# VectorE's 32x32 block transposes for the input rows and the first layer's row terms, in a two-layer graph-attention and expert kernel

## The chip, the cores and the metric

The kernel runs on one core of one Trainium2 chip, as one launch. The metric is device time in microseconds, first instruction to last; lower is better. A core has five engines that each run their own list of instructions in order and wait for one another through semaphores: TensorE (PE in the profile, with PEld for its weight loads), VectorE (DVE), ScalarE (ACT), GpSimd (POOL) and SyncE (SP), which here only issues DMAs.

## The reference: what is computed

`x` has 64 batches of 256 rows and 256 columns in f32; `adj` is one 256x256 mask for all of them. Each batch goes through two layers:

```python
# layer 0
x = x + elu(gat4(layernorm(x), adj, W0, a0))     # 4 heads of 64, slope 0.2
x = x + layernorm(x) @ weight.T + bias
# layer 1
x = x + relu(gat1(layernorm(x), adj, W1, a1))    # 1 head of 256, slope 0.01
x = x + moe(layernorm(x))                        # 8 experts, the best 2 of each row
```

Attention of a head, with `q = h @ W`:

```python
e = leaky_relu((q @ a_src)[:, None] + (q @ a_dst)[None, :])   # one term per row, one per column
p = softmax(where(adj, e, -inf), axis=-1)
out = p @ q
```

The expert stage adds `moe(n) = n + sum of the two chosen experts' gelu(n @ w1 + b1) @ w2 + b2`, each weighted by its share.

## The kernel before

**Layout.** Rows lie on the 128 partitions: a batch is a tile of 128 partitions, 2 row halves (NT) and 256 columns. A matmul needs its contracted dimension on the partitions, so before every projection the batch is transposed to 2 column halves (KT) on partitions by 256 rows.

**One batch** (`batch_layers`, L370). It takes its rows from `xin`, issues the load of the batch three further on (`load_batch`, L93, one 256 KB DMA on SyncE's queue), takes statistics (`norm_stats`, L286: VectorE's mean and variance, then GpSimd's `rstd`), and transposes (`transposed`, L297: four 128x128 transposes on TensorE into a PSUM bank, which ScalarE copies out at L305). `projected` (L308) multiplies with `wx0`; the centring of the layer norm is folded into the weights, and `rstd` comes in afterwards as a scale. Each head has three more columns beside its 64 (columns 64 to 66): the attention terms. L323 takes their exponentials on ScalarE, L327 scales q on VectorE.

**Scores without a softmax pass.** `scores` (L333) uses that an exponential of a sum is a product and a leaky ReLU is a maximum, so that a score before normalisation is `max(row term, column term) * mask`, the other factors being in q or cancelling. The row term must run along the free dimension, the same on all partitions. L339 gets it by transposing column `d+1` of q, broadcast to 128 columns, on TensorE: 8 transposes a batch in layer 0 (4 heads, 2 halves), 2 in layer 1. L346 makes `z` from it on VectorE. Layer 0 does two heads in one step, two in the next. `attended` (L352) multiplies `z` with q on TensorE and divides by the sum, which is q's extra column.

**The rest of the batch.** elu and the residual (L394 to L398, `ex` and `x1`), the linear layer (L401 to L417, with `x1b` as residual plus bias), the second attention (L420 to L434, with `rel`), the last norm, and the router's logits (L472). Rows go to `xs` in DRAM by expert through indirect DMAs on GpSimd (`send`, L739, `route`, L758), come back in pairs of tiles (`expert_pair`, L584), pass two matmuls (`hidden`, `result`) and are added to `out` by indirect DMAs (`scatter`, L675).

**What sets the order.** The program order is written out by hand (L898 on). A batch is a generator that yields a rank; a step of the outer loop runs one piece of every active job, sorted by rank. A batch starts every third step, so about six are in flight, and what one piece makes is mostly used in the next step. Every engine keeps that order. In ranks: the load, the statistics of x0 and its transpose are at 40; the projection at 20; heads 0 and 1 at 10; heads 2 and 3 at 10; `attended` at 50. Expert pieces come at 90, 40, 30 and 80, indirect DMAs at 95 and 97.

**Buffers.** The eight PSUM banks are handed out in turn by `bank` (L78). SBUF tiles share slots by tag: `e`, `x1b` and `rel` have two each, `xT` four, `xin` six.

Of the kernel before, what the change touches and what calls it, by code (L numbers as in the profile page):

```python
# [26 lines left out]
def kernel(  # L27
# [69 lines left out]
        )  # L97
        return t

    AHEAD = 3  # L100
    xin = {0: load_batch(0)}


# [3 lines left out]
    nc.vector.memset(ones, 1.0)  # L107
    mean_w = const.tile([P, P], F32, tag="mean_w", name="mean_w")
    nc.vector.memset(mean_w, 1.0 / D)
    mhalf = const.tile([P, NT], F32, tag="mhalf", name="mhalf")  # L110
    nc.vector.memset(mhalf, -0.5)

# [26 lines left out]
    def gnn_weights(w, a, heads, slope, name):  # L139

        d = D // heads
        wx = const.tile([P, KT, heads, d + 3], F32, tag=name, name=name)
        for k in range(KT):
            nc.sync.dma_start(
                out=wx[:, k, :, :d],  # L150
                in_=w[k * P : (k + 1) * P, :].rearrange("p (h d) -> p h d", h=heads),
            )
        av = work.tile([P, 2, d], F32, tag="e", name=name + "_a")
        nc.scalar.dma_start(out=av.rearrange("p s d -> p (s d)"), in_=rows_to_all(a, 2 * d))
        prod = work.tile([P, heads, d], F32, tag="hp", name=name + "_p")
        for k in range(KT):
            for s, c in ((0, d + 1), (1, d)):
                nc.vector.tensor_mul(
                    prod, wx[:, k, :, :d], av[:, s : s + 1, :].to_broadcast([P, heads, d])
                )  # L160
                nc.vector.tensor_reduce(wx[:, k, :, c : c + 1], prod, AX.X, ALU.add)
            nc.vector.tensor_scalar(
                wx[:, k, :, d + 1 : d + 2], wx[:, k, :, d + 1 : d + 2], 1.0 - slope, None,
                op0=ALU.mult,
            )
            nc.vector.tensor_scalar(
                wx[:, k, :, d + 2 : d + 3], wx[:, k, :, d : d + 1], slope - 1.0, None,
                op0=ALU.mult,
            )
        flat = wx.rearrange("p k h c -> p k (h c)")  # L170
        center(flat, heads * (d + 3))
        return flat
# [2 lines left out]
    wx1 = gnn_weights(w1g, a1g, 1, SLOPE1, "wx1")  # L175

    wf_in = work.tile([P, KT, D], F32, tag="xT", name="wf_in", bufs=4)
    xin.update({b: load_batch(b) for b in range(1, AHEAD)})
    nc.scalar.dma_start(out=wf_in, in_=wf.rearrange("(t p) i -> p t i", p=P))
    wfT = const.tile([P, KT, D], F32, tag="wfT", name="wfT")  # L180
# [10 lines left out]
    nc.scalar.dma_start(out=bias_f, in_=rows_to_all(bf, D))  # L191
    nc.vector.tensor_scalar(bias_f, bias_f, -1.0, None, op0=ALU.add)

    r_in = work.tile([E, D], F32, tag="x1b", name="r_in")
    nc.scalar.dma_start(out=r_in, in_=router)
    rT = const.tile([P, KT, E], F32, tag="rT", name="rT")
    pr = bank("pr", [KT, E])
# [132 lines left out]
            )  # L330
        return q

    def scores(q, heads, hs, mask, probs):  # L333

        d = D // heads
        pd = bank("pd", [len(hs), N])
        for i, h in enumerate(hs):
            for t in range(NT):
                nc.tensor.transpose(  # L339
                    pd[:, i, t * P : (t + 1) * P],  # L340
                    q[:, t, h, d + 1 : d + 2].to_broadcast([P, P]), ident,
                )
        for i, h in enumerate(hs):
            z = work.tile([P, NT, N], F32, tag="z", name="z", bufs=6)
            for j in range(NT):
                nc.vector.scalar_tensor_tensor(  # L346
                    z[:, j, :], pd[:, i, :], q[:, j, h, d + 2 : d + 3], mask[:, j, :],
                    op0=ALU.max, op1=ALU.mult,
                )
            probs.append(z)  # L350
# [19 lines left out]
    def batch_layers(b, c0, xng, lg):  # L370

        x0 = xin.pop(b)
        if b + AHEAD < B:
            xin[b + AHEAD] = load_batch(b + AHEAD)
        _, rstd = norm_stats(x0)
        xT = transposed(x0)
        yield 20
        q = projected(xT, wx0, H, rstd)
        yield 10
        probs = []  # L380
        scores(q, H, range(0, 2), masks[0], probs)
        yield 10
        scores(q, H, range(2, 4), masks[0], probs)
        yield 50
        pvs, rinv = attended(q, H, probs)
        hp = work.tile([P, NT, D], F32, tag="hp", name="hp")
        for t, pv in enumerate(pvs):
            nc.vector.tensor_tensor(
                hp[:, t, :].rearrange("p (h d) -> p h d", h=H), pv[:, :, :HD],
                rinv[:, t, :, None].to_broadcast([P, H, HD]), ALU.mult,  # L390
            )
        yield 20
        ex = work.tile([P, NT, D], F32, tag="e", name="e")
        nc.scalar.activation(ex, hp, AF.Exp)  # L394

        x1 = work.tile([P, NT, D], F32, tag="x1", name="x1", bufs=2)
        nc.vector.scalar_tensor_tensor(x1, hp, 0.0, x0, op0=ALU.max, op1=ALU.add)
        nc.vector.scalar_tensor_tensor(x1, ex, 1.0, x1, op0=ALU.min, op1=ALU.add)  # L398
        yield 30
        x1b = work.tile([P, NT, D], F32, tag="x1b", name="x1b")  # L400
        nc.gpsimd.tensor_add(x1b, x1, bias_f[:, None, :].to_broadcast([P, NT, D]))  # L401
        _, rstd = norm_stats(x1)
        xT = transposed(x1)
        yield 70
        pf = bank("pf", [NT, D])
        for t in range(NT):
            for k in range(KT):
                nc.tensor.matmul(  # L408
                    pf[:, t, :], xT[:, k, t * P : (t + 1) * P], wfT[:, k, :],
                    start=(k == 0), stop=(k == KT - 1),  # L410
                )
        x2 = work.tile([P, NT, D], F32, tag="x2", name="x2", bufs=4)
        for t in range(NT):
            nc.vector.scalar_tensor_tensor(
                x2[:, t, :], pf[:, t, :], rstd[:, t : t + 1], x1b[:, t, :],
                op0=ALU.mult, op1=ALU.add,
            )  # L417
        _, rstd = norm_stats(x2)
        yield 60
        xT = transposed(x2)  # L420
        yield 20
        q = projected(xT, wx1, 1, rstd)
        yield 10
        probs = []
        scores(q, 1, range(1), masks[1], probs)
        yield 40
        pvs, rinv = attended(q, 1, probs)
        yield 5
        rel = work.tile([P, NT, D], F32, tag="rel", name="rel")
        for t, pv in enumerate(pvs):  # L430
            nc.scalar.activation(  # L431
                rel[:, t, :], pv[:, 0, :D], AF.Relu, scale=rinv[:, t, :]
            )
        nc.gpsimd.tensor_add(x2, x2, rel)  # L434
        yield 60
        mv, rstd = norm_stats(x2)
        yield 15

        by = small.tile([P, 2, NT], F32, tag="by", name="by")
        nc.vector.scalar_tensor_tensor(  # L440
            by[:, 0], mv[:, :, 0], -1.0, rstd, op0=ALU.mult, op1=ALU.mult
        )
        nc.vector.tensor_scalar(by[:, 1], rstd, 1.0, None, op0=ALU.add)
        yield 50
        xe = keep.tile([P, NT, ROW], F32, tag="xng", name="xng", bufs=XNG)
        dense = b >= ROUTED
        base = work.tile([P, NT, D], F32, tag="dbase" if dense else "base", name="base")
        for t in range(NT):
            nc.scalar.activation(
                xe[:, t, :D], x2[:, t, :], AF.Identity, bias=by[:, 0, t : t + 1],  # L450
                scale=rstd[:, t : t + 1],
            )
        for t in range(NT):
            nc.scalar.activation(
                base[:, t, :], x2[:, t, :], AF.Identity, bias=by[:, 0, t : t + 1],
                scale=by[:, 1, t : t + 1],
            )
        xng.append(xe)
        yield 35
        if not dense:  # L460
            d = nc.sync.dma_start(
                out=out_rows[b * N : (b + 1) * N, :].rearrange("(t p) d -> p t d", p=P), in_=base
            )
            tc.declare_no_dep(
                d.ins, query=SYNC, group="out", reason="no row is added to before its chunk has been sent"
            )
            tc.add_to_no_dep_group("out", d.ins)
            based.append(d.ins)
            nc.sync.nop()
        xT = transposed(xe[:, :, :D], *(("xTd", DENSE) if dense else ()))  # L470
        yield 50
        pl = bank("pl", [NT, E])  # L472
        for t in range(NT):
            for k in range(KT):
                nc.tensor.matmul(
                    pl[:, t, :], xT[:, k, t * P : (t + 1) * P], rT[:, k, :],
                    start=(k == 0), stop=(k == KT - 1),
                )
        nc.vector.tensor_copy(lg[:, c0 : c0 + NT, :], pl)
        if dense:  # L480
            dense_batch[b] = dict(base=base, xT=xT)
# [480 lines left out]
```

## Time and profile before

| | |
|---|---|
| median of three runs | 1795.14 us |
| lowest, highest | 1784.11, 1803.95 us |
| profiled execution | 1821.2 us |
| granted TensorE clock in it | 0.937 of full |
| DMA | 192.90 MB in 137374 packets, mean 106 GB/s |

The profile's rows and the shares below are from the execution of 1821.2 us. A row of its costliest groups reads: line, engine, operation, tile written and tiles read, shape, count; then busy time and mean length in ns; then the idle time of the engine ahead of these instructions and what ended it. Groups that the change touches (total busy time, and mean length of one):

| line | engine | what | count | busy us | mean ns |
|---|---|---|---|---|---|
| L301 | PE | transposes of x0 (`pt<-ident,xin`) | 256 | 39.8 | 280 |
| L301 | PE | transposes of x1, x2 and the normed rows | 768 | 119.8 | 277 |
| L339 | PE | transposes of the row terms, both layers | 640 | 106.0 | 281 |
| L305 | ACT | copies of the transposed rows | 256 | 144.9 | 589 |
| L346 | DVE | z | 640 | 265.1 | 473 |

Busy times of TensorE are sums of overlapping records; what a group of them takes in the engine's order has to be read from start to start in the timeline. Three stages follow one another: until about 270 us batches with little expert work beside them, until about 1450 us batches and experts together, then experts alone.

### The profile page before, as it was taken

The numbers are of one execution on the slowest core, as the hardware profiler recorded it, in microseconds if no ns is written. First come the engines' busy times: TensorE is split into PE (matmuls) and PEld (weight loads), VectorE is DVE, ScalarE is ACT, GpSimd is POOL, SyncE is SP. The second block draws the span as 40 slices with busy tenths as digits, with TensorE's granted clock in tenths as the row PEclk, the third lists the DMA queues.
The fourth block names the chain that finished last, engine by engine and source line by source line (L and its number), as shares of the span: only waits on it lengthen the run. The fifth ranks groups of instructions, "written<-read, shape, count | busy, mean of one in ns | idle before, by whom it ended". The sixth has DMA issues, their size and how long they took to land. (4 is left out here: it accounts for less than half of the span.)

```text
span 1821.2 us, 30155 instructions
## 1 busy us (share of the span) xinstructions
PE 1629.5 (89%) x9254; PEld 1433.0 (79%) x9254; DVE 1231.4 (68%) x4680; ACT 839.9 (46%) x1773; POOL 1084.2 (60%) x1164
## 2 busy tenths in 40 slices
PE   6998889899999999999999999999989998778692
PEld 5787778788888888888878788887878887667582
DVE  6889887867685858686766768688678876522231
ACT  1243333355554555554545545555455545443241
POOL 1333645557575767767676757576685767644444
PEclk9999989899998999998989999999899989889897
DMA  4410211235344444544354534444353436576663
GB/s 137 140 36 24 71 60 53 79 109 121 105 95 104 109 126 108 132 103 110 93 119 112 119 91 95 118 111 128 84 127 101 107 82 166 118 186 139 135 139 43
DMA packets 137374, 192.90 MB, mean 106 GB/s; under 512 B 18680, under 2 KB 91392, under 8 KB 137216
## 3 DMA queue, kind: packets, MB, share of 16 engines
q1 hardware_dynamic: 86592, 122.61, 22.0%
q0 software_dynamic: 49632, 67.39, 20.6%
q8 instruction: 76, 1.25, 0.3%
q10 hardware_dynamic: 992, 0.99, 0.2%
q14 instruction: 82, 0.67, 0.1%
HBM read 101.77 MB, written 89.15 MB: 105 GB/s over the span
## 5 line engine op out<-in xcount | busy, mean ns | idle before, releaser
L681 POOL DMA_INDIRECT out_dram<-y,to x262 | 419.4, 1601 | 231.1 <-DMA out_dram<-y,to 103.5
L360 PE MATMUL pv<-q,z 128*128 128x65 f32 (+1 forms) x2560 | 394.4, 314 | 5.3 <-DVE z L346 5.0
L360 PEld LDWEIGHTS pv<-q,z 128*128 128x128 f32 x2560 | 364.9, 210 | 21.1 <-DVE z L346 5.4
L293 POOL TENSOR_SCALAR rstd<-mv 128x2 f32<-128x2 f32 x256 | 81.2, 317 | 376.2 <-DVE mv L291 355.6
L741 POOL DMA_INDIRECT xs<-xng,pos x248 | 261.2, 1053 | 68.2 <-issue 66.0
L315 PE MATMUL pq<-wx,xT 128*128 128x268 f32 (+1 forms) x1024 | 265.4, 402 | 35.8 <-ACT xT L305 31.8
L649 PE MATMUL ph<-sT,we 128*128 128x256 f32 x1048 | 252.6, 397 | 48.1 <-ACT sT L621 22.9
L346 DVE SCALAR_TENSOR_TENSOR z<-pd,q,mask 128x256 f32<-128x256 f32 x640 | 265.1, 473 | 9.9 <-PE pd L339 7.5
L649 PEld LDWEIGHTS ph<-sT,we 128*128 128x128 f32 x1048 | 205.0, 200 | 80.6 <-ACT sT L621 29.4
L664 PE MATMUL py<-w2s,hT 128*128 (+1 forms) x1176 | 265.4, 381 | 0.6 <-ACT hT L655 0.6
L315 PEld LDWEIGHTS pq<-wx,xT 128*128 128x128 f32 x1024 | 188.1, 194 | 85.8 <-ACT xT L305 50.6
L664 PEld LDWEIGHTS py<-w2s,hT 128*128 128x128 f32 x1176 | 220.5, 191 | 29.3 <-ACT hT L655 1.0
L305 ACT COPY xT<-pt 128x512 f32<-128x512 f32 x256 | 144.9, 589 | 192.8 <-PE pt L301 127.6
L327 DVE SCALAR_TENSOR_TENSOR q<-pq,rstd,q 128x256 f32<-128x256 f32 x256 | 112.4, 479 | 154.5 <-ACT q L323 150.7
L655 ACT ACTIVATE hT<-ph,we 128x256 f32<-128x256 f32 x294 | 123.3, 471 | 173.4 <-PE ph L649 122.9
L670 DVE TENSOR_TENSOR y<-py,b2s 128x512 f32<-128x512 f32 x147 | 96.7, 688 | 149.2 <-PE py L664 77.9
L294 POOL TENSOR_TENSOR rstd<-rstd,mhalf 128x2 f32<-128x2 f32 x256 | 184.2, 719 | 21.4
L642 ACT ACTIVATE y<-y,w 128x256 f32<-128x256 f32 x262 | 112.9, 498 | 177.5 <-DVE y L670 171.1
L290 DVE BATCH_NORM_STATS2 stats<-x 128x6 f32<-128x256 f32 x384 | 155.9, 406 | 0.0
L408 PE MATMUL pf<-wfT,xT 128*128 128x256 f32 x512 | 145.7, 435 | 0.1
L323 ACT ACTIVATE q<-pq,rstd 128x12 f32<-128x12 f32 (+1 forms) x256 | 56.5, 265 | 162.3 <-POOL rstd L294 150.8
L434 POOL TENSOR_TENSOR x<-x,rel 128x512 f32<-128x512 f32 x64 | 109.2, 1706 | 25.2 <-ACT rel L431 25.0
(147 smaller groups left out, 2259.2 us busy)
## 6 DMA issues: line engine op xcount, KB each, us to landing
we<-wpack SPq DMA_DIRECT2D x147, 288.0 KB
xr<-xs SPq DMA_DIRECT2D x131, 260.0 KB
xin<-in_x_dram SPq DMA_DIRECT2D x64, 256.0 KB
out_dram<-base SPq DMA_DIRECT2D x64, 256.0 KB
out_dram<-y,to POOLq DMA_INDIRECT x262
xs<-xng,pos POOLq DMA_INDIRECT x248
xs<-fill SPq DMA_DIRECT2D x9, 260.0 KB
wpack<-wt SPq DMA_DIRECT2D x8, 288.0 KB
```

The lines of the kernel that those rows point to most:

```text
L290: nc.vector.bn_stats(stats[:, t, :], src[:, t, :])
L294: nc.gpsimd.tensor_tensor(rstd, rstd, mhalf, ALU.pow)
L305: nc.scalar.copy(dst, pt)
L315: nc.tensor.matmul(pq.rearrange("p h c -> p (h c)"), xT[:, k, t * P : (t + 1) * P], wx[:, k, :], start=(k == 0), stop=(k == KT - 1),)
L346: nc.vector.scalar_tensor_tensor(z[:, j, :], pd[:, i, :], q[:, j, h, d + 2 : d + 3], mask[:, j, :], op0=ALU.max, op1=ALU.mult,)
L360: nc.tensor.matmul(pv[:, h, :], z[:, j, t * P : (t + 1) * P], q[:, j, h, : d + 1], start=(j == 0), stop=(j == NT - 1),)
L408: nc.tensor.matmul(pf[:, t, :], xT[:, k, t * P : (t + 1) * P], wfT[:, k, :], start=(k == 0), stop=(k == KT - 1),)
L649: nc.tensor.matmul(ph[:, f, :], we[:, k * D + f * P : k * D + (f + 1) * P], xT[:, k, :], start=(k == 0), stop=(k == KT - 1),)
L655: nc.scalar.activation(hT[:, f, :], ph[:, f, :], AF.Gelu, bias=we[:, C_B1 + f : C_B1 + f + 1])
L664: nc.tensor.matmul(py[:, t, :], hT[:, f, t * P : (t + 1) * P], w2s[:, e, f * D : (f + 1) * D].rearrange("p e c -> p (e c)"), start=(f == 0 ...
L681: d = nc.gpsimd.indirect_dma_start(out=out_rows, out_offset=bass.IndirectOffsetOnAxis(ap=to[:, t : t + 1], axis=0), in_=y[:, t, :], in_off ...
L741: d = nc.gpsimd.indirect_dma_start(out=xs_d[: E * CAP * PAIR, :], out_offset=bass.IndirectOffsetOnAxis(ap=at, axis=0), in_=xe, in_offset=None,
```

## The change

It takes two sorts of transposes from TensorE and gives them to VectorE, whose transpose instruction turns each 32x32 block where it stands and moves no block to another place. Both places are arranged so that this is enough.

**The rows of x0.** `load_blocks` loads the batch a second time, with every 32x32 block already at its transposed place but not turned: four DMAs of 32 partitions each, in runs of 32 elements (128 B). One VectorE transpose of 128x512 then gives `xT`. The row-major load stays, since statistics and residual use it. Two batches are loaded ahead into three buffers.

**The row terms of layer 0.** `quadrants` multiplies the row term of each head by a mask of the column groups (`quad`), which spreads it to 32 columns (4 heads, 2 halves, 4 groups). `shared` multiplies that on TensorE with a matrix of ones where the partition agrees modulo 32 (`peers`): afterwards partition `32g + j` holds the terms of all rows `32c + j`, for every g. VectorE copies this out of PSUM (`rs`), and transposes it, broadcast over 32 columns, straight into the PSUM bank `pd`, for two heads at a time. Layer 1 keeps its TensorE transposes.

**Room for it.** The buffers of `e`, `x1b` and `rel` go from two to one.

```diff
+    def load_blocks(b):
+        t = io.tile([P, KT, N], F32, tag="xblk", name=f"xblk_{b}", bufs=3)
+        for g in range(P // S):
+            nc.sync.dma_start(
+                out=t[g * S : (g + 1) * S].rearrange("q k (c a) -> q k c a", a=S),
+                in_=x[b].rearrange("(c q) (k g a) -> g q k c a", q=S, g=P // S, a=S)[g],
+            )
+        return t
+
+    S = 32
+    AHEAD, BLOCKS_AHEAD = 3, 2
+    xblk = {0: load_blocks(0)}
     xin = {0: load_batch(0)}
...
+    quad = const.tile([P, G], F32, tag="quad", name="quad")
+    nc.vector.tensor_reduce(quad, ident.rearrange("p (g a) -> p g a", a=S), AX.X, ALU.add)
+    peers = const.tile([P, G, S], F32, tag="peers", name="peers")
+    nc.vector.tensor_reduce(
+        peers[:, 0, :], ident.rearrange("p (g a) -> p a g", a=S), AX.X, ALU.add
+    )
+    for g in range(1, G):
+        nc.vector.tensor_copy(peers[:, g, :], peers[:, 0, :])
...
+    xblk.update({b: load_blocks(b) for b in range(1, BLOCKS_AHEAD)})
     xin.update({b: load_batch(b) for b in range(1, AHEAD)})
...
+    def quadrants(q):
+        rq = small.tile([P, H, NT, G], F32, tag="rq", name="rq")
+        nc.vector.tensor_tensor(
+            rq, q[:, :, :, HD + 1 : HD + 2].rearrange("p t h o -> p h t o").to_broadcast([P, H, NT, G]),
+            quad[:, None, None, :].to_broadcast([P, H, NT, G]), ALU.mult,
+        )
+        return rq
+
+    def shared(rq):
+        pr = bank("pr", [H, NT * G])
+        nc.tensor.matmul(
+            pr.rearrange("p h c -> p (h c)"), peers.rearrange("p g a -> p (g a)"),
+            rq.rearrange("p h t g -> p (h t g)"), start=True, stop=True,
+        )
+        rs = small.tile([P, H, NT * G], F32, tag="rs", name="rs")
+        nc.vector.tensor_copy(rs, pr)
+        return rs
+
+    def scores(q, heads, hs, mask, probs, rs=None):
         d = D // heads
         pd = bank("pd", [len(hs), N])
-        for i, h in enumerate(hs):
+        if rs is not None:
+            nc.vector.transpose(
+                pd.rearrange("p h n -> p (h n)"),
+                rs[:, hs[0] : hs[-1] + 1, :, None].to_broadcast([P, len(hs), NT * G, S]),
+            )
+        for i, h in enumerate(hs if rs is None else ()):
             for t in range(NT):
                 nc.tensor.transpose(
...
         _, rstd = norm_stats(x0)
-        xT = transposed(x0)
+        xb = xblk.pop(b)
+        if b + BLOCKS_AHEAD < B:
+            xblk[b + BLOCKS_AHEAD] = load_blocks(b + BLOCKS_AHEAD)
+        xT = work.tile([P, KT, N], F32, tag="xT", name="xT", bufs=4)
+        nc.vector.transpose(xT.rearrange("p k n -> p (k n)"), xb.rearrange("p k n -> p (k n)"))
         yield 20
         q = projected(xT, wx0, H, rstd)
+        rq = quadrants(q)
         yield 10
         probs = []
-        scores(q, H, range(0, 2), masks[0], probs)
+        rs = shared(rq)
+        scores(q, H, range(0, 2), masks[0], probs, rs)
         yield 10
-        scores(q, H, range(2, 4), masks[0], probs)
+        scores(q, H, range(2, 4), masks[0], probs, rs)
...
-        ex = work.tile([P, NT, D], F32, tag="e", name="e")
+        ex = work.tile([P, NT, D], F32, tag="e", name="e", bufs=1)
...
-        x1b = work.tile([P, NT, D], F32, tag="x1b", name="x1b")
+        x1b = work.tile([P, NT, D], F32, tag="x1b", name="x1b", bufs=1)
...
-        rel = work.tile([P, NT, D], F32, tag="rel", name="rel")
+        rel = work.tile([P, NT, D], F32, tag="rel", name="rel", bufs=1)
```

More of the change, by code (lines that the diff above doesn't have):

```diff
@@ L98, in load_batch @@
         return t
-    AHEAD = 3
+    def load_blocks(b):
[9 more added lines that the diff above has]
+    xblk = {0: load_blocks(0)}
     xin = {0: load_batch(0)}
@@ L109 @@
     nc.vector.memset(mean_w, 1.0 / D)
+    G = P // S
+    quad = const.tile([P, G], F32, tag="quad", name="quad")
[6 more added lines that the diff above has]
+        nc.vector.tensor_copy(peers[:, g, :], peers[:, 0, :])
     mhalf = const.tile([P, NT], F32, tag="mhalf", name="mhalf")
@@ L152, in gnn_weights @@
             )
-        av = work.tile([P, 2, d], F32, tag="e", name=name + "_a")
+        av = work.tile([P, 2, d], F32, tag="e", name=name + "_a", bufs=1)
         nc.scalar.dma_start(out=av.rearrange("p s d -> p (s d)"), in_=rows_to_all(a, 2 * d))
@@ L192 @@
     nc.vector.tensor_scalar(bias_f, bias_f, -1.0, None, op0=ALU.add)
-    r_in = work.tile([E, D], F32, tag="x1b", name="r_in")
+    r_in = work.tile([E, D], F32, tag="x1b", name="r_in", bufs=1)
     nc.scalar.dma_start(out=r_in, in_=router)
@@ L331, in projected @@
         return q
-    def scores(q, heads, hs, mask, probs):
+    def quadrants(q):
[15 more added lines that the diff above has]
+    def scores(q, heads, hs, mask, probs, rs=None):
         d = D // heads
         pd = bank("pd", [len(hs), N])
-        for i, h in enumerate(hs):
+        if rs is not None:
[4 more added lines that the diff above has]
+        for i, h in enumerate(hs if rs is None else ()):
             for t in range(NT):
```

## The prediction

> **What bounds the kernel now.** I read the page's engine totals first, then busy time by stage, then the waits of VectorE inside the long stage, and last the timeline for the prices. The totals:
>
> ```profile
> PE 1629.5 (89%) x9254; PEld 1433.0 (79%) x9254; DVE 1231.4 (68%) x4680; ACT 839.9 (46%) x1773; POOL 1084.2 (60%) x1164
> ```
>
> TensorE leads, VectorE is next. Cut by stage (columns: length; busy time and count of PE, PEld, DVE, ACT, POOL; granted clock; DMA share; GB/s):
>
> ```profile
> 90.00:270.00 180.00, 159.92 (x964) 138.51 (x962) 155.64 (x547) 63.40 (x152) 83.88 (x120) 0.94 0.15 48
> 270.00:1450.00 1180.00, 1115.58 (x6515) 989.77 (x6515) 859.48 (x3271) 608.30 (x1258) 785.13 (x846) 0.95 0.43 105
> ```
>
> The same stages for the z tiles alone show 100 and 474 VectorE instructions. A batch makes 10 of them, so the early stage handles 10 batches at 18.0 us each, the long one 47.4 at 24.9 us. In the long stage TensorE is busy 95% and VectorE 73%; in the early stage, before the experts have work, 89% against 86%. After 1450 us the batches are over and nothing of the change is left. So a saving on TensorE counts 47 times where VectorE has room, and about 15 times where it has little. How much room, the waits of VectorE in the long stage say:
>
> ```profile
> DVE q L327 <- ACT q L323: 126.6, 62, 6.5
> DVE rinv L367 <- PE pv L360: 97.2, 76, 3.2
> DVE x L414 <- PE pf L408: 13.7, 10, 1.6
> DVE lg L479 <- PE pl L475: 10.6, 17, 0.6
> DVE z L346 <- PE pd L339: 7.5, 9, 1.5
> ```
>
> All its waits there add up to 281 us, 5.9 us a batch. Those on PE (the last four, with py 4.0 and pq 2.3) are 135 us, 2.9 us a batch: VectorE has caught up with TensorE, and work put there is free. Those on ACT are 2.7 us a batch, 127 us in all. The page puts the ACT wait behind them on the 12-column form of L323 (the first layer) and on GpSimd's rstd. The rest of the period, 24.9 - 5.9 = 19.0 us, VectorE is occupied (18.1 busy, 0.9 between instructions). In the early stage its waits are 13.1 + 4.8 us, so 16.2 of 18.0 us are occupied. TensorE itself waits some 63 us in the long stage, mostly on ACT's xT, sT and on loads, hardly on VectorE.
>
> [...] The trace has no VectorE transpose[...]. TensorE's 128x128 f32 transposes show 273 ns each, but overlap. [...] The block loads come in runs of 128 B. The nearest here is wx in 256 B runs, queue q1 from 4.0 to 5.2 us:
>
> ```profile
> q1 hardware_dynamic: 264, 0.07, 24.4%
> ```
>
> 0.244 x 16 engines x 1.2 us / 264 = 17.7 ns a packet[...].
>
> **The change part by part.** TensorE, from the timeline (start, length, engine, line, operation):
>
> ```profile
> 901.99 0.33 PE L769 MATMUL pp<-m,tri 128*128 128x64 f32 x2
> ...
> 902.16 0.39 PE L770 MATMUL pp<-m,ones 128*128 128x64 f32 x2
> ...
> 902.38 0.60 PE L339 MATMUL pd<-ident,q 128*128 128x128 f32 x4
> ...
> 912.04 0.60 PE L301 MATMUL pt<-ident,x 128*128 128x128 f32 x4
> ...
> 912.48 0.60 PE L301 MATMUL pt<-ident,xin 128*128 128x128 f32 x4
> ...
> 912.91 3.62 PE L664 MATMUL py<-w2s,hT 128*128 x16
> ```
>
> Four transposes hold TensorE 0.43 us start to start, 0.11 us each. Gone per batch: 4 of x0 and 8 of the row terms, 12 x 0.11 = 1.32 us. Added: one f32 matmul of 32 columns; pp with 64 columns takes 0.17 to 0.22 us, I take 0.20. Net 1.12 us a batch, 72 us over 64; 53 of them in the long stage.
>
> ScalarE loses one 128x512 copy, 589 ns a batch. It is 52% idle there, so I count nothing.
>
> VectorE gains three transposes of 128x512. Lower bound 0.42 us each (the 128x512 maskf conversion, the fastest such row), upper 1.38 us[...]. I take 0.69: 2.07 us. Two small instructions (the 32-column product, the copy of 32 columns out of PSUM) cost 0.18 us each like `lg` and `rinv`. Sum 2.43 us a batch, 156 us in all; range 1.6 to 4.5.
>
> Where it lies: the x0 transpose stands in rank 40 behind x0's statistics, and the first layer's q of the next step comes later on VectorE. So its 0.69 us goes into the 2.7 us that q waits for rstd: GpSimd starts on rstd at the statistics, not at the transpose. The other 1.74 us must fit into the waits on PE, which shrink from 2.9 to 2.9 - 1.12 = 1.8 us. It just fits. Queued behind the two pd transposes are the z instructions of the same slot; TensorE wants z one or two steps later, a step being 8.3 us, so a delay of 1 us passes.
>
> Two new waits. The copy of `rs` waits for the small matmul, first on TensorE in its step as the pd transposes were; those cost VectorE 7.5 us in all. The pd transposes write a PSUM bank, so VectorE now waits for that bank; the order of banks (17 a batch) is unchanged, and its user lies eight allocations back. Both near nothing.
>
> Loads: 2048 packets a batch x 17.7 ns / 16 = 2.3 us, 145 us over the run, 8% on top of the long stage's 43% share; at 35 ns 16%. They are issued two batches, 50 us, ahead. SyncE issues four DMAs more, 0.4 to 0.6 us each, about 2 us of 24.9; the weight loads queued behind them run a step ahead. Hidden. The single buffers of e, x1b and rel are free two steps before their next use: hidden too.
>
> Start: the first block load stands ahead of xin and wx on the queue, about 2 us, and the masks of ones take some 1 us on VectorE: +3 us.
>
> **Sum.** Long stage: of 1.12 us I count 0.95, since VectorE is then nearly full: 47.4 x 0.95 = -45 us. Early: VectorE needs 16.2 + 2.43 = 18.6 us against 18.0, +0.6 us over 15 batches = +9. Start +3. Total -33: 1795 - 33 = 1762 us.
>
> **Rivals.**
> - Gain given back. With both engines over 90% full, bursts (routing puts several us of small instructions on VectorE once a chunk) make TensorE wait for z, x1 or q. Half the gain stays in the long stage, -21; early a batch costs 16.2 + 2.43 + 0.6 of the ACT wait = 19.2, +18; start +3: 1795 us. For it: the early stage at 86%. Against it: TensorE hardly waits on VectorE today.
> - VectorE bounds, slower. The ACT waits stay whole and `rs` adds 0.5 us: 19.0 + 2.43 + 2.7 + 0.5 = 24.6 us, only -14; early 16.2 + 2.43 + 1.3 + 0.5 = 20.4, +36; start +5: 1822 us. For it: 127 us of waits come through GpSimd, which is not relieved. Against it: rstd is asked for before the new work.
> - Transposes at half rate, 1.38 us. Long stage 19.0 + 4.5 + about 2 = 25.5, +30; early 16.2 + 4.5 + 0.65 = 21.4, +50; start +3: 1878 us. [...] No row here shows it.
>
> **How the numbers follow.** Forecast 0.50, given back 0.22, VectorE bounds 0.20, half rate 0.08. The time is the forecast's. About a seventh of the forecast's chance lies above 1777 us (faster by less than 1%), so faster 0.45; same takes that and most of the second case, 0.25; slower 0.30. The range goes from 1735 (the whole 53 us, with the early stage unharmed) to 1835, past the VectorE case; half rate and the ends of the others, under 0.2, stay out.
>
> **What would show it.** Transposes at 0.6 to 0.75 us; TensorE's busy time down by some 70 to 100 us of records; VectorE near 1390 us; its waits on pv in the long stage down from 97 to under 40 us while those on ACT shrink less; the early stage longer by several us, the long one shorter by some 45; DMA packets up by 131,072, with no new waits on `we` or `xr`. I am wrong if TensorE gains waits on z, q or x1, if a transpose takes over 1 us, or if the rs copy waits more than 0.5 us a batch.

## The result and the profile after

The kernel became slower by 11.9%: 2008.16 us (median of 4, 2008.01 to 2011.23) against 1797.05 us before in the same comparison (1784.11 to 1803.95). The ratio is 1.1188, with a 95% interval of 1.1123 to 1.1253. The forecast was 1762 us, with a range up to 1835.

The profiled execution of the kernel before, 1821.2 us, was 1.3% longer than this median; where the start times of batches are compared below, I use the kernel of run e7_loads_only in its place, which does the same arithmetic in the same order and took 1798.6 us in its profile.

The engine totals of the page after:

```profile
PE 1582.0 (79%) x8614; PEld 1376.3 (69%) x8614; DVE 1387.6 (69%) x5005; ACT 812.6 (40%) x1709; POOL 1088.8 (54%) x1164
```

TensorE lost 47 us of busy time and VectorE gained 156, as planned for VectorE, but now neither is above 79%: the lost time is idle time on both. The same stages as before, cut at the same times (columns: start and end; length; busy time and count of PE, PEld, DVE, ACT, POOL; granted clock; DMA share; GB/s):

```profile
90.00:270.00 180.00, 121.16 (x623) 101.39 (x622) 127.29 (x410) 41.75 (x102) 48.31 (x75) 0.81 0.19 47
270.00:1450.00 1180.00, 976.85 (x5586) 858.59 (x5587) 907.35 (x3217) 532.29 (x1108) 718.38 (x783) 0.93 0.44 105
```

In the early stage TensorE falls from 159.9 to 121.2 us busy and VectorE from 155.6 to 127.3, and the granted clock from 0.94 to 0.81. The z tiles of the two stages count 78 and 453 instructions, ten to a batch: 23.1 us a batch in place of 18.0, and 26.0 in place of 24.9. By the start times of the batches' statistics, against e7_loads_only: batches 0 to 20 took 494.3 us in place of 374.8 (+119.5), batches 20 to 63 1129.6 in place of 1048.0 (+81.6), and what follows +7. Three waits of the whole kernel name the place (engine, tile and line that wait, what released them; us in total, times, longest):

```profile
POOL rstd L317 <- DVE mv L315: 493.7, 93, 24.7
...
PE pq L339 <- DVE xT L429: 238.9, 52, 11.8
...
DVE rinv L416 <- PE pv L409: 182.9, 139, 4.8
```

TensorE waits 239 us for `xT`, the tile that VectorE now makes, 52 times in 64 batches, and 162.5 of these us lie in the long stage. VectorE in turn waits for TensorE's `pv`, 182.9 us where it was 114.7. GpSimd's wait for the statistics was 355.6 us before; I read its growth as the same lateness seen from a third engine. The group of projections on the page, before and after (busy us and mean ns of one, then the idle time ahead of it):

```profile
L315 PE MATMUL pq<-wx,xT 128*128 128x268 f32 (+1 forms) x1024 | 265.4, 402 | 35.8 <-ACT xT L305 31.8
L339 PE MATMUL pq<-wx,xT 128*128 128x268 f32 (+1 forms) x1024 | 328.1, 474 | 296.2 <-DVE xT L429 238.9
```

Before, nearly all of the idle time was for ScalarE's copy. The mean matmul rose from 402 to 474 ns although its shape is unchanged. The new transposes are what I priced, by the list of groups, and by the view of one tile (min/median/max ns, first and last start):

```profile
L382 DVE STREAM_TRANSPOSE pd<-rs 128x512 f32<-128x512 f32 x128 | 92.6, 724 | 3.1
```

```profile
L429 DVE STREAM_TRANSPOSE xT<-xblk x64: 693/711/712, 13.7 to 1635.2; 128x512 f32<-128x512 f32 x64
```

One step of the early stage in the timeline after (start, length, engine, line, operation; in brackets the idle time before and what ended it) shows the loop:

```profile
124.17 0.39 DVE L314 BATCH_NORM_STATS2 stats<-xin 128x6 f32<-128x256 f32 x1
...
124.78 0.71 DVE L429 STREAM_TRANSPOSE xT<-xblk 128x512 f32<-128x512 f32 x1
...
125.63 3.91 PE L339 MATMUL pq<-wx,xT 128*128 128x268 f32 x8 [4.54 <-DVE xT L429]
...
129.87 3.68 PE L409 MATMUL pv<-q,z 128*128 128x65 f32 x32
...
133.59 0.18 DVE L416 RECIPROCAL rinv<-pv 128x4 f32<-128x4 f32 x1 [1.60 <-PE pv L409]
...
146.25 0.39 DVE L314 BATCH_NORM_STATS2 stats<-xin 128x6 f32<-128x256 f32 x1
...
146.85 0.71 DVE L429 STREAM_TRANSPOSE xT<-xblk 128x512 f32<-128x512 f32 x1
```

The transposition starts as the statistics end, without a wait, and the loads of its blocks had been issued by 77 us: it is VectorE's turn that came late. TensorE starts the projection at 125.63, does `pq` and then `pv`, and only at 133.59 can VectorE take `rinv`. From there to the end of the next transposition at 147.56 VectorE works through its list. The two stretches cut out:

```profile
125.63:133.59 7.96, 7.96 (x45) 6.98 (x46) 1.86 (x6) 1.13 (x3) 0.25 (x1) 0.75 0.26 50
133.59:147.56 13.97, 8.14 (x44) 6.44 (x43) 13.48 (x43) 4.79 (x11) 5.80 (x10) 0.97 0.10 31
```

In the first TensorE is busy without a break and VectorE 1.86 us; in the second VectorE 13.48 of 13.97 us, and TensorE ends it idle for 4.5 us. Together 21.9 us, which is the step: for much of it one engine waits for the other, where they had worked side by side. At the same place of the kernel before:

```profile
129.30 2.07 PE L315 MATMUL pq<-wx,xT 128*128 128x268 f32 x8 [0.56 <-ACT xT L305]
...
130.08 0.40 DVE L290 BATCH_NORM_STATS2 stats<-xin 128x6 f32<-128x256 f32 x1
```

TensorE and ScalarE had turned and projected a batch's rows before VectorE came to that batch's statistics at all, and the step was 15.67 us (the next `pq` at 144.97). TensorE's list ran ahead of VectorE's, and this lead is what the change took away.

### The profile page after: what moved, and what is told of

Same layout as the page of the kernel before. It is cut to its first block, busy times and chain, and to the rows that moved or that the text cites. A ratio compares the mean times of both kernels' runs of the same rounds, so it can differ in the third digit from the quotient of the medians.

```text
span 2006.5 us, 29544 instructions
## 1 busy us (share of the span) xinstructions
PE 1582.0 (79%) x8614; PEld 1376.3 (69%) x8614; DVE 1387.6 (69%) x5005; ACT 812.6 (40%) x1709; POOL 1088.8 (54%) x1164
## 2 busy tenths in 40 slices
DMA packets 272543, 209.66 MB, mean 104 GB/s; under 512 B 153848, under 2 KB 226560, under 8 KB 272384
## 5 line engine op out<-in xcount | busy, mean ns | idle before, releaser
L339 PE MATMUL pq<-wx,xT 128*128 128x268 f32 (+1 forms) x1024 | 328.1, 474 | 296.2 <-DVE xT L429 238.9
L339 PEld LDWEIGHTS pq<-wx,xT 128*128 128x128 f32 x1024 | 223.9, 230 | 365.5 <-DVE xT L429 205.5
L409 PE MATMUL pv<-q,z 128*128 128x65 f32 (+1 forms) x2560 | 368.4, 300 | 0.0
L409 PEld LDWEIGHTS pv<-q,z 128*128 128x128 f32 x2560 | 341.2, 197 | 13.7
L796 POOL DMA_INDIRECT xs<-xng,pos x248 | 269.1, 1085 | 68.2 <-issue 60.9
L329 ACT COPY xT<-pt 128x512 f32<-128x512 f32 x192 | 112.7, 587 | 184.0 <-PE pt L325 183.2
L416 DVE RECIPROCAL rinv<-pv 128x4 f32<-128x4 f32 (+1 forms) x256 | 39.0, 169 | 183.1 <-PE pv L409 182.9
L314 DVE BATCH_NORM_STATS2 stats<-x 128x6 f32<-128x256 f32 x384 | 155.6, 405 | 0.0
L449 ACT ACTIVATE e<-hp 128x512 f32<-128x512 f32 x64 | 40.3, 630 | 222.7 <-DVE hp L443 222.7
```

The lines of the kernel that those rows point to most:

```text
L314: nc.vector.bn_stats(stats[:, t, :], src[:, t, :])
L339: nc.tensor.matmul(pq.rearrange("p h c -> p (h c)"), xT[:, k, t * P : (t + 1) * P], wx[:, k, :], start=(k == 0), stop=(k == KT - 1),)
L409: nc.tensor.matmul(pv[:, h, :], z[:, j, t * P : (t + 1) * P], q[:, j, h, : d + 1], start=(j == 0), stop=(j == NT - 1),)
L796: d = nc.gpsimd.indirect_dma_start(out=xs_d[: E * CAP * PAIR, :], out_offset=bass.IndirectOffsetOnAxis(ap=at, axis=0), in_=xe, in_offset=None,
```

## The experiments

My theory: **the lead is lost**. A producer that TensorE needs early now stands in VectorE's list behind work that TensorE needs late. Rivals: the work that VectorE gained; the block loads; the transpose operation as such; TensorE's low clock. A second question came up on the way: with the lead restored, why is there still no gain?

| run | ratio to before | 95% interval |
|---|---|---|
| the change itself | 1.119 | 1.112 to 1.125 |
| e1_hoist | 1.012 | 1.007 to 1.018 |
| e2_scores_only | 1.017 | 1.010 to 1.023 |
| e3_x0_only | 1.070 | 1.064 to 1.076 |
| e4_vector_copy | 1.063 | 1.058 to 1.069 |
| e5_turn_first | 1.085 | 1.079 to 1.091 |
| e6_filler | 1.112 | 1.106 to 1.119 |
| e7_loads_only | 1.0005 | 0.998 to 1.003 |
| e8_late20 | 1.009 | 1.006 to 1.012 |
| e9_relief20 | 1.0004 | 0.998 to 1.003 |
| e10_added_only20 | 1.005 | 1.002 to 1.008 |
| e11_late20_order | 0.999 | 0.996 to 1.002 |
| e12_early_order | 1.015 | 1.010 to 1.020 |
| e13_relief_pool | 0.978 | 0.973 to 0.983 |
| e14_relief_vector | 0.998 | 0.995 to 1.002 |
| e15_relief_both | 0.980 | 0.976 to 0.984 |
| e16_no_relief | 0.974 | 0.969 to 0.980 |

### Where the loss comes from

**e1_hoist: the whole change, each batch's blocks turned one slot earlier.**

```diff
+    def turn(b):
...
+        t = work.tile([P, KT, N], F32, tag="xT0", name="xT0", bufs=2)
...
+        turned[b] = t
+        if b + BLOCKS_AHEAD < B:
+            xblk[b + BLOCKS_AHEAD] = load_blocks(b + BLOCKS_AHEAD)
...
-        xT = work.tile([P, KT, N], F32, tag="xT", name="xT", bufs=4)
-        nc.vector.transpose(xT ..., xb ...)
...
+        if b + 1 < B:
+            turn(b + 1)
+        xT = turned.pop(b)
```

> The changed kernel, but VectorE turns the blocks of batch b+1 in the slot of batch b, three steps before TensorE wants them; same VectorE work, same loads, xT for the other transposes with three slots, a tag of its own with two for the first. Theory (queue place): xT is made behind the statistics in VectorE's queue, TensorE wants it there and then, and the two engines go in lock-step in the early stage; taken away, 1770 to 1830 us. Rival A (VectorE's 2.4 us a batch are too much): stays at 1960 to 2010. Rival B (the loads in 128 B runs, late or in the way): stays at 1960 to 2010.

1833.45 us, a little above the range; the kernel before took 1812.09 us beside it, and the ratio is 1.012. The same VectorE work, the same loads, and nine tenths of the loss are gone (0.106 of 0.119). TensorE's longest waits in this kernel:

```profile
PE ph L715 <- DMA we<-wpack: 52.5, 20, 14.0
PE pq L339 <- ACT xT L329: 41.7, 57, 1.0
```

No wait on VectorE's `xT` is left among them, and in the timeline the first layer's `pq` starts at 129.25, 145.06 and 160.87, without a wait ahead of it:

```profile
129.25 1.97 PE L339 MATMUL pq<-wx,xT 128*128 128x268 f32 x8
...
145.06 1.97 PE L339 MATMUL pq<-wx,xT 128*128 128x268 f32 x8
```

That is 15.8 us a step, against 22.0 in the changed kernel and 15.7 before. So the place in the list is the cause, not the amount of work.

**e3_x0_only and e2_scores_only: one half of the change each.** In the first the row terms stay with TensorE; in the second x0 does.

```diff
# e3_x0_only
-        rq = quadrants(q)
...
-        rs = shared(rq)
-        scores(q, H, range(0, 2), masks[0], probs, rs)
+        scores(q, H, range(0, 2), masks[0], probs)
# e2_scores_only
-        nc.vector.transpose(xT ..., xb ...)
+        xT = transposed(x0)
```

> Only x0 goes to VectorE, with the block loads; row terms on TensorE as before. Theory (queue place): the lock-step stays, 1930 to 2000 us. Rival A (VectorE load, here 0.7 of 2.4 us a batch): 1830 to 1870. Rival B (loads): 1960 to 2010.

> Only the row terms go to VectorE; x0 is transposed on TensorE as before, no block loads. Theory (queue place): no lock-step, 1775 to 1815 us. Rival A (VectorE load, here 1.75 of 2.4 us a batch): 1910 to 1960. Rival B (loads): 1775 to 1815.

x0 alone gave 1941.02 us (1.070), the row terms alone 1837.26 us (1.017). The loss sits with x0:

```profile
PE pq L339 <- DVE xT L429: 195.1, 52, 11.9
```

The halves add up to 8.7% and the whole is 11.9%. My reading, not tested: in the loop the row terms' two transposes, at 137.44 and 141.53 us in the timeline above, lie in VectorE's stretch of the step and lengthen it in full; without the loop part of them lies beside other work. The row terms alone came out a little above the theory's upper end.

**e4_vector_copy: the kernel before, VectorE copying x0's transposes out of PSUM.** TensorE keeps its transposes; no blocks, no 32x32 transposition.

```diff
-        xT = transposed(x0)
+        xT = transposed(x0, copy=nc.vector.tensor_copy)
```

> The kernel before, with one edit: the copy of x0's transposes out of PSUM is made by VectorE in place of ScalarE, at the place in VectorE's queue where the changed kernel has its transpose. No block loads, no VectorE transposes, nothing taken from TensorE. Theory (queue place): lock-step as with the change, 1930 to 2010 us. Rival A (VectorE load, 0.7 us a batch): 1830 to 1870. Rival B (loads): 1795 within 1%.

1925.41 us, ratio 1.063, just below what the theory gave, and far from 1795. Moving one 128x512 copy from ScalarE, 46% busy in the kernel before, to VectorE does nearly all of the damage of moving x0's transposition there:

```profile
PE pq L315 <- DVE xT L305: 175.0, 54, 12.2
```

So it is neither the transposition nor the loads. It is whose list `xT` stands in, and where.

**e5_turn_first: the change, with the transposition ahead of x0's statistics in its own slot.**

```diff
-        _, rstd = norm_stats(x0)
         xb = xblk.pop(b)
...
         nc.vector.transpose(xT ..., xb ...)
+        _, rstd = norm_stats(x0)
```

> The changed kernel with the x0 transpose put ahead of the statistics of its own slot, which moves it 2.3 us forward in VectorE's queue and changes nothing else. Theory (queue place): the wait of TensorE per batch shrinks from 4.5 to about 2.3 us, over some 22 batches, and less of it runs at half clock: 50 to 100 us less than the changed kernel, ratio to the kernel before 1.06 to 1.09. Rivals (VectorE load, loads): no change, ratio 1.11 to 1.125.

1941.89 us, ratio 1.085. The statistics that it passes are 1.1 us long, not the 2.3 that I had expected; TensorE's wait ahead of the projection fell in the early steps from 4.52 to 3.47 us, and 3.4 of the 11.9% were won. A lead of these few instructions left 8.5 of the 11.9%; one of a whole slot, in e1_hoist, left 1.2.

**e6_filler: nine matmuls, read by nobody, ahead of the projection in the first 24 batches,** so that TensorE isn't idle while it waits.

```diff
+        if b < 24:
+            pk = bank("pk", [D])
+            for _ in range(9):
+                nc.tensor.matmul(pk, mean_w, wfT[:, 0, :], start=True, stop=True)
         q = projected(xT, wx0, H, rstd)
```

> The changed kernel with nine matmuls of no use (128x256, some 4.4 us in all) ahead of the first projection of batches 0 to 23; they are there to fill TensorE's wait for xT, so that its clock stays up. Theory, with the halved clock as a part of the loss (the projection takes 3.9 in place of 2.0 us after such a wait): 25 to 45 us less than the changed kernel, ratio 1.095 to 1.105. If the wait alone counts: no gain or some loss, ratio 1.115 to 1.14.

1991.59 us, ratio 1.112: between the two expectations. The projection after the wait went back to its old length:

```profile
141.63 2.07 PE L339 MATMUL pq<-wx,xT 128*128 128x268 f32 x8 [0.64 <-DVE xT L429]
```

The step there shrank from 22.0 to 20.1 us, and the mean granted clock of the profiled execution rose from 0.903 in the changed kernel to 0.938. Between the profiles of the two kernels lie 19.8 us, between the ratios 0.6%, some 11 us. From these I estimate that in these batches the low clock after the wait (0.50 in the cut of the changed kernel below) adds 11 to 20 us to the loss, less than the 25 to 45 of the theory; it comes with the loop and is no cause of its own.

**e7_loads_only: the block loads, the single buffers and the masks, with nothing turned by VectorE.**

```diff
-        xT = work.tile([P, KT, N], F32, tag="xT", name="xT", bufs=4)
-        nc.vector.transpose(xT ..., xb ...)
+        xT = transposed(x0)
```

> The kernel before with the change's block loads, its single buffers and its masks of ones, and none of its transposes: the blocks are loaded and not used. Theory (queue place): only the later start, ratio 1.000 to 1.008. Rival B (loads in 128 B runs in the way): 1.03 or more.

1792.25 us, ratio 1.0005. The 131,072 small packets cost nothing beyond the interval of 0.3%.

### Why there is no gain once the lead is back

**e8_late20 and e11_late20_order: the first 20 batches as before, then the change with the blocks turned a slot early.** Late batches have the experts' work beside them, where I had counted on TensorE's relief. The second issues the block loads ahead of the transposition of the same slot, into a buffer freed a batch ago.

```diff
# e11_late20_order against e8_late20
+        if 20 <= b + BLOCKS_AHEAD < 64:
+            xblk[b + BLOCKS_AHEAD] = load_blocks(b + BLOCKS_AHEAD)
         if 20 <= b + 1 < 64:
             turn(b + 1)
-        if 20 <= b + BLOCKS_AHEAD + 1 < 64:
-            xblk[b + BLOCKS_AHEAD + 1] = load_blocks(b + BLOCKS_AHEAD + 1)
```

> A version that should beat both: the first 20 batches as before, on TensorE; from batch 20 on the change, with the x0 transpose three steps early as in e1. Theory: the start and the early stage cost nothing, the long stage gains 0.65 to 0.85 us a batch over some 40 batches: ratio 0.978 to 0.990. If the change gains nothing in the long stage either: 1.00 to 1.01.

> As the run with the change from batch 20 on (ratio 1.009), but the loads of the turned blocks are issued one place earlier, into a buffer freed a batch ago, so SyncE does not stand on VectorE's turn with the experts' weights queued behind it. If that wait of SyncE (240 us there in the long stage) ate the gain, ratio 0.980 to 0.992 and the waits of TensorE for we fall from 23 us to near nothing. If VectorE's added work ate it, ratio 1.003 to 1.010 as before.

e8_late20 gave 1.009, a clear miss: I had expected 0.978 to 0.990. Its trace named a suspect, SyncE standing on VectorE with the experts' weight loads behind it (480 to 1250 us):

```profile
SPq L105 <- DVE y L733: 190.1, 24, 12.8
SPq L105 <- DVE xT L424: 52.1, 8, 7.9
```

e11_late20_order removed these waits and with them TensorE's 22.9 us of waits for `we` in that stretch, and gave 0.999, between my two ranges. So the wait, my own edit's, had cost about 1%; but the gain did not appear either.

**e9_relief20: from batch 20 on TensorE's 12 transposes left out, with nothing in their place.** ScalarE's copy of x0's transposes goes with them. This is more relief than the change can give.

```diff
-        xT = transposed(x0)
+        xT = still if 20 <= b < 64 else transposed(x0, "xT0", 2)
...
-        pd = bank("pd", [len(hs), N])
+        pd = bank("pd", [len(hs), N]) if rs is None else rs
```

> From batch 20 on the 12 TensorE transposes of x0 and of the first layer's row terms are left out and nothing stands in their place: projection and scores read a constant tile, so the output is not the reference's. This asks what TensorE's relief is worth by itself in the long stage. If TensorE sets the pace there, 44 batches x 12 x 0.11 us = 58 us, ratio 0.965 to 0.980. If the pace there is set by the chain of a batch through the engines, or by VectorE, ratio 0.990 to 1.002, with TensorE idle longer by what was taken out.

Ratio 1.0004: as it ran, the relief brought nothing. Batches 20 to 60 in e7_loads_only and here:

```profile
385.10:1360.00 974.90, 935.97 (x5601) 831.21 (x5600) 730.35 (x2776) 530.10 (x1095) 685.82 (x728) 0.98 0.53 125
```

```profile
383.30:1352.60 969.30, 891.43 (x5120) 786.77 (x5118) 728.08 (x2777) 509.01 (x1054) 693.22 (x728) 0.97 0.46 114
```

TensorE lost 44.5 us of busy time and the 40 batches took 5.6 us less. Most of the rest turned into waits, TensorE's in the same stretch, first with the transposes and then without:

```profile
PE pq L339 <- ACT xT L329: 13.2, 48, 0.3
...
PE ph L701 <- ACT sT L673: 3.9, 10, 0.4
```

```profile
PE pq L340 <- ACT xT L330: 29.2, 40, 0.7
PE ph L704 <- ACT sT L676: 22.0, 10, 5.3
```

I read this so: the removed transposes had filled time in which TensorE would otherwise wait for ScalarE's copy of an earlier transposition, and the 96% busy share had hidden that. The busy time of TensorE's weight loads, 831 of 975 us, is higher than any other engine's too, and still leaving transposes out did not shorten the kernel.

One rival is not ruled out. In the 29 executions of the kernel before that the ratio of this run rests on, the time follows the granted clock, by some 16 us for 0.01 of clock. The kernel without the transposes ran at a mean clock of 0.940, the kernel before at 0.948. By that slope, an estimate, up to 13 us of a gain can lie hidden under the lower clock. Whether the clock fell because TensorE waited more often, and so whether that is a price of the relief, no run separates. It is at most a quarter of the 58 us forecast where TensorE sets the pace.

**e10_added_only20: VectorE's three transposes added from batch 20 on, read by nobody; TensorE keeps its own.**

```diff
+        if b >= 20:
+            nc.vector.transpose(spare ..., still ...)
         xT = transposed(x0, "xT0", 2)
```

> From batch 20 on VectorE turns three constant 128x512 tiles into a spare tile at the three places of the change, and nobody reads them; TensorE keeps all its transposes. This asks what VectorE's added 44 x 3 x 0.7 = 92 us cost by themselves. If VectorE has room there (busy 75%), ratio 1.000 to 1.005. If the turns stand ahead of work that TensorE soon wants, each of the some 2 us a batch passes on in part: ratio 1.015 to 1.045.

Ratio 1.005. VectorE has room in the long stage: 92 us of added work cost about 9 (3 to 14 by the interval). It is not what ate the gain.

**e12_early_order: the change in all batches but two, the blocks turned a slot early, loads in the better order.**

```diff
# against e11_late20_order
-        if 20 <= b + 1 < 64:
+        if 2 <= b + 1 < 64:
             turn(b + 1)
```

> The change in all batches but the first two, each block turned in the slot of the batch before and the loads issued early as in the run beside it. The first hoisted version gave 1.012. With SyncE's wait gone: 0.990 to 1.005 if that wait mattered, 1.008 to 1.015 if what is left is VectorE's added work in the early batches, which the start times of the batches put at some 30 us over the first twenty.

Ratio 1.015, the upper case. Between this profile and that of e11_late20_order lie 21.9 us, 16.4 of them in batches 0 to 20. I read this as VectorE's added work, paid for in the early stage, where both engines were 86 to 89% busy before, even with the lead restored; no run adds that work alone to the early batches.

**e13_relief_pool to e16_no_relief: is the step of 24 us GpSimd's or VectorE's?** From batch 20 on: TensorE's relief with GpSimd's two adds left out as well (e13), with half of VectorE's first-layer score products left out as well (e14), with both (e15), and both without TensorE's relief (e16).

```diff
-        nc.gpsimd.tensor_add(x1b, x1, bias_f[:, None, :].to_broadcast([P, NT, D]))
+        if b < 20:
+            nc.gpsimd.tensor_add(x1b, x1, bias_f[:, None, :].to_broadcast([P, NT, D]))
+        else:
+            x1b = x1
...
-        nc.gpsimd.tensor_add(x2, x2, rel)
+        if b < 20:
+            nc.gpsimd.tensor_add(x2, x2, rel)
...
-            for j in range(NT):
+            for j in range(rows):
```

> From batch 20 on TensorE's 12 transposes are left out as in the relief run (which gave 1.000), and so are GpSimd's two adds of 1.85 us a batch (the bias is not added to x1, the second layer's result not to x2). If GpSimd's order of adds and scatters held the step at 24.2 us, the relief now counts: ratio 0.960 to 0.980. If the round trips or VectorE hold it: 0.993 to 1.003.

> TensorE's 12 transposes left out from batch 20 on, and half of VectorE's score products of the first layer with them (4 x 0.47 us a batch; both halves of the sum read the one that is made). If VectorE's work between two TensorE steps held the step: ratio 0.960 to 0.980. If GpSimd or the ScalarE copies hold it: 0.993 to 1.003.

> TensorE's transposes, GpSimd's adds and half of VectorE's first-layer score products left out from batch 20 on. If one of the two engines held the step, as the better of the two runs beside it, and less than 0.98. If neither did, and TensorE's short waits for ScalarE's copies (67 us in the relief run over 40 batches) hold it: 0.985 to 1.000.

> GpSimd's adds and half of VectorE's first-layer score products left out from batch 20 on, TensorE keeps all its transposes. If TensorE is bound as soon as the others have room, this stays at 0.990 to 1.003 while the run with the relief goes lower. If TensorE was never the bound, this goes as low as that one.

Taking GpSimd's adds out shortens the kernel by 2.0 to 2.6% in all three kernels that do it. Taking VectorE's products out as well as TensorE's transposes does nothing (0.998). And e16_no_relief, where TensorE keeps every transpose, is no slower than e15_relief_both, which drops them (0.974 and 0.980, intervals that overlap). Its page:

```profile
PE 1598.6 (91%) x9254; PEld 1411.5 (80%) x9254; DVE 1155.9 (66%) x4510; ACT 837.5 (48%) x1773; POOL 969.9 (55%) x1076
```

So an engine with a lower busy share, GpSimd, has work whose removal shortens the kernel. That it sets the step, as the ranges set beforehand would have it, is not shown. By the start times of the batches (us; the last column runs from the start of batch 63 to the end of the kernel):

| run | batches 20 to 40 | batches 40 to 60 | from batch 63 on |
|---|---|---|---|
| e7_loads_only | 478.9 | 496.0 | 365.6 |
| e9_relief20 | 473.5 | 495.7 | 368.5 |
| e13_relief_pool | 480.0 | 475.0 | 357.9 |
| e15_relief_both | 483.1 | 481.9 | 355.7 |
| e16_no_relief | 476.7 | 475.5 | 355.3 |

In batches 20 to 40 leaving out the adds brought nothing, with TensorE's relief or without. The gain comes in batches 40 to 60 and after the last batch has begun, where hardly an add is left to leave out. GpSimd's adds also lie both in its list, among the scatters, and on a batch's own way from layer to layer, and without them the router sees other values, though the counts of expert matmuls and of scatters stay the same. The clock muddles the comparison of e15 and e16 too: 0.937 against 0.953 on average, which by the slope above is some 25 us in favour of e16, more than the 10 us between their medians, so that pair can't show that the relief is worth nothing beside GpSimd's. What sets the step in the long stage stays open.

## Why the prediction was wrong

**Prices: right.** Three transposes at 0.71 to 0.73 us against 0.69, my estimate from the 128x512 f32 instructions that VectorE already had (L397, L398 and L670 of the kernel before, means of 685 to 692 ns); the copy of `rs` 0.16 against 0.18; VectorE 1387.6 us against "near 1390". Half rate, the case of 1878 us, was an estimate too, twice those 0.69 us, for which the kernel before gave no ground; at 0.71 to 0.73 us it is ruled out. The copy of `rs` waited 0.6 us in all. DMA packets rose by 135,169 (137,374 to 272,543), where I expected 131,072. TensorE's records fell by 47 us, not 70 to 100: the longer `pq` matmuls alone gave 63 us back (328.1 against 265.4).

**Loads, buffers, single copies: right.** e7_loads_only puts them at 1.0005. Queue q1's share went from 22.0% of 1821.2 us to 28.6% of 1798.6 us in that kernel: 114 us of 16 engines, by this estimate 13 ns a packet, against my 17.7. The 17.7 came from runs of 256 B; that it would hold for runs of 128 B was an assumption of mine. The short runs were no concern here: at 1.0005 the transfers are hidden. The start was underrated: the first projection ran at 27.7 us in place of 20.2, where I said +3; in e7_loads_only it ran at 29.9, and that kernel is no slower than the one before.

**"Where it lies": the step that failed.** I wrote that x0's transpose "goes into the 2.7 us that q waits for rstd". I asked who comes after it on VectorE, and not who reads its result, and when. The reader is TensorE's projection, which ran ahead of VectorE's statistics of the same batch. So the sum put x0's transpose at no time of its own, and the reader's wait was no term of it at all. "I am wrong if TensorE gains waits on z, q or x1" guarded the wrong tiles: the wait came on `xT`, 238.9 us. What I should have put beside it is the order of VectorE's list: in the trace the transposition at 124.78, whose loads were issued by 77 us, starts only behind the statistics of 124.17. The cost of this one step is the difference between the change and e1_hoist, 10.6%, about 191 of the 211 us.

**The early stage, apart from the loop: undersized, a small term.** +9 us forecast for VectorE's fullness; e12_early_order against e11_late20_order puts it at 22 between the profiles and 29 between the ratios.

**The long stage, -45 us: wrong too.** I took the engine that is 95% busy for the bound, and its relief for time won. VectorE's waits for `pv` there, which I expected to fall from 97 to under 40 us, rose to 122.8. e9_relief20 shows that 12 transposes fewer gave nothing (ratio 1.0004, 0.998 to 1.003): 44.5 us of work became 39 us of other time, mostly waits, with the clock as the open remainder. "A saving on TensorE counts 47 times" is the sentence that fell. The -45 would have been close to 0 even with the lead kept (e11_late20_order, 0.999). No version of the change that I ran beat the kernel before.

**The rivals.** None held 2008 us. "Given back" was nearest for the long stage (half of the gain, where none came), with routing bursts as a reason that no run tested; "VectorE bounds" had the right sign by luck: e10_added_only20 shows that VectorE takes the work in the long stage for 0.5%.

## What to carry to other kernels

When an operation moves to another engine, look up its reader's start beside the start of the neighbours it will have in the new engine's list: here the reader ran ahead of them, the two engines fell into step, and a step of 15.7 us became a stretch of one engine plus a stretch of the other (7.96 and 13.97 us), for an operation of 0.71 us. Give such a producer its lead back by issuing it for the next item, one step early, with a buffer that is already free (here the ratio went from 1.119 to 1.012 in e1_hoist, and from 1.009 to 0.999 in e11_late20_order by the free buffer). And a busy share of 96% didn't say what a relief was worth (1.0004 in e9_relief20): leave the work out in one run before you price it.

## What I had not expected of the hardware

After 4.54 us without work TensorE's first projection took 3.91 us in place of 2.07, and the cut of 126.50 to 128.00 us shows a granted clock of 0.50:

```profile
126.50:128.00 1.50, 1.50 (x5) 1.06 (x4) 0.00 (x0) 0.14 (x1) 0.00 (x0) 0.50 0.53 83
```

All seven first-layer projections of the changed kernel from 90 to 270 us stand behind waits of 4.52 to 11.48 us and took 3.72 to 3.94 us; with the filler the idle time was 0.64 us and the same projection took 2.07. Shorter waits were followed by the low clock too. In the kernel before, after a wait of 2.08 us, TensorE ran at a granted clock of 0.50 for 10.3 us, with work to do, and 32 matmuls that take 3.69 us at 131.65 took 6.93:

```profile
842.50:852.80 10.30, 10.17 (x42) 9.75 (x43) 3.92 (x19) 3.82 (x8) 5.52 (x9) 0.50 0.61 137
842.63 1.09 PE L617 MATMUL px<-ident,xr 128*128 128x128 f32 x4 [2.08 <-DMA xr<-xs]
843.51 6.93 PE L360 MATMUL pv<-q,z 128*128 128x65 f32 x32
```

In that kernel's timeline from 20 to 1450 us TensorE has 16 waits of 1.85 to 3.69 us, and within 4 us of the end of each the granted clock stood at 0.50; of 11 waits of 0.84 to 1.49 us two were followed so. What sets the clock, this doesn't show. The 32 matmuls took 3.24 us more than at 131.65, which is longer than the wait of 2.08 us ahead of them. VectorE's transposition of 128x512 f32 went straight into PSUM at 0.73 us, from a broadcast source, against 0.71 into SBUF.
